# A graph network's passage from its first layers to its third: late adjacency slabs behind the last row, their indices apart, and another first node tile

## The chip, the core and the metric

The kernel runs on one core of a Trainium2 chip. The core has five engines with an instruction queue each: TensorE (PE) for matmuls, VectorE (DVE), ScalarE (ACT), GpSimd (POOL, which here issues mostly indirect gathers) and SyncE (SP, which here issues most of the DMAs). Within a queue the order is fixed; between queues, semaphores hold an instruction until what it needs is there. The metric is the time of one execution in microseconds (us), lower is better; the median of several runs is compared.

## What is computed

There are N = 2708 nodes with D = 512 features each and a sparse 2708 x 2708 adjacency with values. Four layers follow each other, each a normalization (subtract the mean, divide by the deviation), a Relu, a graph operation and a residual addition:

```
x = x + L0(relu(norm(x)), adj)   # inc = adj + (adj>0)/|row|;  inc @ h / row sum of inc
x = x + L1(relu(norm(x)), adj)   # 8-head attention, scores - 1e16 * (1 - max(adj, I)), softmax
x = x + L2(relu(norm(x)), adj)   # relu(adj @ (h W1) + b1); relu(adj @ (. W3) + b3); tanh(. Wf + bf)
x = x + L3(relu(norm(x)), adj)   # mean of (h W + b) over the nonzero neighbours
```

The term of 1e16 in layer 1 outweighs the scores, so the softmax picks the neighbour with the largest value in the row of `max(adj, I)`. The kernel uses this: with y = relu(norm(x)) Wv Wo for all nodes, layer 1 is a gather of one row of y per node. It checks by flags that this holds, and has a general path behind them for the case that it doesn't.

## The kernel before

Nodes are handled in 22 tiles of 128 rows (the last has 20). A stretch of 128 rows of the adjacency, 128 x 2708 floats or 1354 KB, is called a slab.

**Layer 0** loops over row tiles m = 0 to 21. A row's sum (`acc`, L810) has a dense part over the first six column tiles (`inc`, made on VectorE in L641 and L649) and a listed part: nonzero rows found by a search, gathered by POOL (L580, L599) and multiplied chunk by chunk (`incl`). VectorE adds the sum to x (`xt`, L826), then come the statistics and the normalization (`norm`, ending in `shift`, L183, and a ScalarE pass `hn`, L186). For layer 1, TensorE transposes `hn` (L192) one row later and multiplies it by the joined weights (`yacc`, L158) two rows later; ScalarE copies the product to `yo` (L756) and SP stores it to `y` (L758).

Beside that each slab goes through passes of its own. On ScalarE: a sign pass and a Relu pass (L527, L528 for late slabs) that count entries. On VectorE, in `attended`: the maximum with the identity (L567), MAX8 (L568) and FIND_INDEX8 (L569), which give the index of the largest entry, `at_top`. The slabs have a ring of three buffers. Six of the slabs, the tiles 3, 4, 5, 0, 1, 2 in this order (`LATE`), are loaded at the start for the row norms alone and loaded again from row m = 14 on, one per row (`load_slab`, L521); their passes follow one row later (`count_signs`, `attended`). A 1x1 copy (`behind`, L164) ties each late sign pass to the row's `xt`.

Ranks of nonzeros for the tiles 1 and 2 are worked out late too: a scan, a store `rank_b` (L387), loads `ranks` (L404), four searches `found` (L420); `ends` (L414) waits for such a load.

After the last row come the copy `idx` of all indices (L861), `degrees` (18 short loads of counts on SP, L338, and 22 short list matmuls, L324), the last two tiles' y and the flags.

**Layer 2** begins with two bias loads (L1072) and `fetch` for the first nine tiles: a load of x into a slot (L1086, SP) and a gather of y by `idx` into another slot (L1088, POOL). Then W3, loaded before, is split into three parts on ScalarE and VectorE (`wb`, L197 to L207), and Wf is loaded (L170). The first output row's loop takes the node tiles 0, 1, 2, ... in order: add the two slots (L1100), store x2 (L1101), normalize, transpose (L923), multiply by W1 (L948), and use the product in the row's own sum (L1032 for the six dense tiles, L1047 for the others).

The order on each engine is not the program's order: a list scheduler with a cost model of its own places the instructions. `issue_after` orders one instruction behind another in that placing, and is no wait on the chip. Memory pools of layer 0 are released before layer 2's are opened, and layer 2's tiles lie over them.

Of the kernel before, what the change touches and what calls it, by code (L numbers as in the profile page):

```python
# [42 lines left out]
def kernel(  # L43
# [92 lines left out]
    idx = const.tile([P, NT], U32, name="idx")  # L136
    BAD_NEG, BAD_MANY, BAD_BOUND = NT, 2 * NT, 3 * NT
    bad = const.tile([P, 3 * NT + 1], FP, name="bad")
    nc.gpsimd.memset(bad, 0.0)
    flag = const.tile([P, 1], I32, name="flag")  # L140
# [32 lines left out]
    def norm(pool, xt, n, dst, func=AF.Identity):  # L173
# [9 lines left out]
        nc.vector.tensor_scalar(  # L183
            shift[:n], mv[:n, 0:1], rstd[:n], -1.0, op0=ALU.mult, op1=ALU.mult
        )
        nc.scalar.activation(dst[:n], xt[:n], func, scale=rstd[:n], bias=shift[:n])  # L186

    def transpose_relu(psum, hn, n, dst):
# [4 lines left out]
        nc.scalar.activation(dst, pt[:, :, :n], AF.Relu)  # L193
# [32 lines left out]
    with tc.tile_pool(name="l0_slab", bufs=2) as slabs, tc.tile_pool(  # L226
# [286 lines left out]
        LATE = FIRST + ZERO  # L513
# [9 lines left out]
        def count_signs(m, last):  # L523

            sgn = slabs.tile([P, N], BF, name="sgn", bufs=GROUP)
            behind(sgn[:1, :1], last)
            nc.scalar.activation(sgn, slab[m], AF.Sign, accum_out=sums_sgn[:, m : m + 1])  # L527
            nc.scalar.activation(sgn, sgn, AF.Relu, accum_out=cnts[:, m : m + 1])  # L528
# [215 lines left out]

        def after(m, hn):

            n = rows(m)
            if hn is not None:
                hTs[m] = wp.tile([P, NCD, P], FP, name="hT")
                transpose_relu(ps_tr, hn, n, hTs[m][:, :, :n])  # L750
                return
# [4 lines left out]
            nc.scalar.copy(yo[:n], yacc[:n])  # L756
# [43 lines left out]
        for m in range(NT):  # L800
# [29 lines left out]
            norm(wp, xt, n, hns[m])  # L830
# [6 lines left out]
            step = m - (NT - 8)  # L837
            if 0 <= step < len(LATE):
                load_slab(LATE[step])
            if 0 < step <= len(LATE):  # L840
                count_signs(LATE[step - 1], xt[:1, :1])
                attended(LATE[step - 1])
# [18 lines left out]
        nc.vector.tensor_copy(idx, at_top[:, :, 0])  # L861
        degrees()
        after(NT - 2, None)
        after(NT - 1, hns.pop(NT - 1))
        after(NT - 1, None)
        flush()
        flags()
# [7 lines left out]

    gp = short.enter_context(tc.tile_pool(name="g", bufs=1))
    wsetb = short.enter_context(tc.tile_pool(name="wsetb", bufs=1))
# [82 lines left out]
    if TAIL:  # L960
        others.append([NFULL])

# [28 lines left out]
    def aggregate(m, parts, shifted, gd, marked):  # L991
# [18 lines left out]
        for ts in dense if dense_of(m) else []:  # L1010
# [13 lines left out]
            for i, t in enumerate(ts):  # L1024
                ghi, glo, gs_ = gs[i]
                first, last = t == 0, t == DENSE - 1
                for acc, a, b, st, sp in (
                    (main, hi, ghi, first, False),
                    (main, lo, glo, False, last),
                    (mixed, s, gs_, first, False),  # L1030
# [789 lines left out]
```

## Time and profile before

| | |
|---|---|
| median of three runs | 1399.31 us (1396.03 to 1404.63) |
| profiled execution | 1402.48 us |
| its span | 1400.7 us |
| mean TensorE clock granted | 0.962 |
| TensorE busy | 1278.7 us (91%) |
| VectorE busy | 932.4 us (67%) |
| ScalarE busy | 689.2 us (49%) |
| POOL busy | 662.4 us (47%) |
| bytes moved | 348.35 MB, mean 249 GB/s |
| loads of slabs | 27, 1354 KB each |
| MAX8 over a slab (L568) | 22, 2.97 us each |
| sign pass of a late slab (L527) | 6, 2.45 us each |

Layer 0 ends and layer 2 begins at about 420 to 490 us of the span. In rows of the trace, the first number is the start, the second the duration, then engine, line, operation, and output <- input; in brackets stands how long the engine was idle before it and what is taken to have ended that. SPq is SP's queue of DMA issues. In the page's rows of 40 digits each digit is the busy share of 35 us in tenths. The rows of a table by windows give start and end, the window's length, then the busy time of PE, PEld (weight loads), DVE, ACT and POOL, the granted clock, the DMA share and GB/s.

### The profile page before, as it was taken

The page shows a single profiled execution, that of the slowest core. Times are in us where ns is not written, and L with a number is a line of the kernel's source. Part 1 is how long each engine was busy: PE and PEld are TensorE (multiplying, and loading weights), DVE is VectorE, ACT ScalarE, POOL GpSimd, SP SyncE. Part 2 cuts the span into 40 slices and gives each one's busy share as a digit, 9 for nine tenths or more (in the row PEclk, how much of TensorE's full clock was granted, in tenths as well). Part 3 has the DMA queues.
Part 4 walks back from the last instruction along what each step waited for, and adds up shares of the span by engine and source line. Part 5 has one row for each costly group of instructions (what it writes and reads, how often), then busy time and mean ns, then how long its engine had stood idle before and what let it go on. Part 6 is the DMA issues. An engine that isn't in the chain of part 4 may idle for free.

```text
span 1400.7 us, 15489 instructions
## 1 busy us (share of the span) xinstructions
PE 1278.7 (91%) x4478; PEld 770.3 (55%) x4478; DVE 932.4 (67%) x1760; ACT 689.2 (49%) x1051; POOL 662.4 (47%) x702
## 2 busy tenths in 40 slices
PE   4889989988887489899999999899999999968997
PEld 2334434434333267556656666466666666646886
DVE  4788999987797688533434446365566656657786
ACT  5887735832444465422333335244455544555553
POOL 2256477778754311265444441333334344635762
PEclk9999999999998799999999999899999999999999
DMA  9999999997884875477777767756555665748994
GB/s 343 359 323 324 316 345 350 318 375 261 295 304 120 306 257 173 161 260 256 247 211 238 239 222 227 240 173 195 170 164 172 197 202 187 243 147 287 301 278 161
DMA packets 188461, 348.35 MB, mean 249 GB/s; under 512 B 22174, under 2 KB 98868, under 8 KB 184636
## 3 DMA queue, kind: packets, MB, share of 16 engines
q1 hardware_dynamic: 140768, 200.13, 42.4%
q0 software_dynamic: 46032, 145.05, 32.1%
q10 hardware_dynamic: 1568, 2.10, 0.4%
q8 instruction: 37, 0.61, 0.2%
q14 instruction: 56, 0.46, 0.1%
HBM read 284.59 MB, written 62.61 MB: 248 GB/s over the span
## 4 chain that ended last, share of the span: by engine, by line
PE 63%; DMA 17%; DVE 9%; issue 4%; ACT 3%; POOL 2%; SPq 0%; DVEq 0%; ACTq 0%; POOLq 0%
PE aggs L1035 15%; PE main L948 10%; PE agg L1032 8%; PE acc L810 6%; DMA h<-h0d,idx_g 5%; PE mixed L948 4%; PE aggs L1032 4%; PE agg L1223 3%; PE aggs L1223 3%; PE pt L923 3%; PE yacc L158 2%; PE aggs L1047 2%; DVE found L420 1%; PE pt L1223 1%; DMA wa<-in_L_gnn_Wo_dram 1%
## 5 line engine op out<-in xcount | busy, mean ns | idle before, releaser
L1035 PE MATMUL aggs<-gg,ac 128*128 128x512 f32 (+1 forms) x520 | 232.4, 594 | 4.3 <-DMA gg<-g1d,idx_g 4.3
L983 POOL DMA_INDIRECT gg<-g2d,idx_g x130 | 131.1, 1009 | 220.5 <-PE aggs L1035 172.0
L983 POOL DMA_INDIRECT gg<-g1d,idx_g x130 | 133.8, 1029 | 173.9 <-PE aggs L1035 103.3
L810 PE MATMUL acc<-h,inc 128*128 128x512 f32 (+1 forms) x348 | 166.5, 629 | 21.2 <-DVE inc L649 21.2
L580 POOL DMA_INDIRECT ac<-in_adj_t_dram,idx_a x130 | 139.2, 1071 | 62.2 <-issue 32.6
L1035 PEld LDWEIGHTS aggs<-gg,ac 128*128 128x128 f32 (+1 forms) x520 | 97.5, 189 | 111.4 <-issue 101.4
L599 POOL DMA_INDIRECT h<-h0d,idx_g x111 | 112.0, 1009 | 56.0 <-issue 38.8
L810 PEld LDWEIGHTS acc<-h,inc 128*128 128x128 f32 (+1 forms) x348 | 67.2, 200 | 103.8 <-issue 77.2
L1019 ACT ACTIVATE a_hi<-raw 128x384 fp32r<-128x384 f32 x84 | 43.5, 520 | 160.9 <-issue 87.8
L1032 PE MATMUL agg<-ghi,a_hi 128*128 128x512 f32 x252 | 115.2, 457 | 1.8 <-ACT a_hi L1019 1.6
L810 PE MATMUL acc<-h,incl 128*128 128x512 f32 (+1 forms) x222 | 104.7, 618 | 8.2 <-DMA h<-h0d,idx_g 8.2
L1032 PE MATMUL agg<-glo,a_lo 128*128 128x512 f32 x252 | 101.9, 404 | 2.4 <-ACT glo L207 2.4
L1032 PE MATMUL aggs<-gs,a_s 128*128 128x512 f32 x252 | 100.4, 401 | 1.1 <-DVE gs L204 1.0
L1020 DVE TENSOR_TENSOR a_lo<-raw,a_hi 128x384 fp32r<-128x384 f32 x84 | 47.3, 563 | 78.4 <-ACT a_hi L1019 50.8
L929 DVE SCALAR_TENSOR_TENSOR v_lo<-pt,v_hi 128x512 fp32r<-128x512 f32 (+1 forms) x88 | 56.7, 665 | 45.2 <-ACT v_hi L928 44.6
L158 PE MATMUL yacc<-wvo,hT 128*128 128x512 f32 (+1 forms) x176 | 82.8, 611 | 1.7 <-ACT hT L193 1.7
L983 POOL DMA_INDIRECT gg<-hidr,idx_h x62 | 62.5, 1009 | 42.8 <-PE aggs L1223 18.2
L910 DVE SCALAR_TENSOR_TENSOR u<-aggs,u 128x512 f32<-128x512 f32 x42 | 28.9, 687 | 76.5 <-PE aggs L1035 75.0
L810 PEld LDWEIGHTS acc<-h,incl 128*128 128x128 f32 (+1 forms) x222 | 41.3, 196 | 57.3 <-issue 39.6
L928 ACT ACTIVATE v_hi<-pt 128x512 fp32r<-128x512 f32 (+1 forms) x88 | 48.6, 578 | 44.1 <-PE pt L923 42.2
L180 ACT ACTIVATE rstd<-mv,eps 128x1 f32<-128x1 f32 x88 | 24.5, 290 | 86.9 <-DVE mv L178 45.3
L568 DVE MAX8 tops<-ar 128x8 f32<-128x2708 f32 (+1 forms) x22 | 65.4, 2972 | 0.1
(326 smaller groups left out, 2787.3 us busy)
## 6 DMA issues: line engine op xcount, KB each, us to landing
ar<-in_adj_dram SPq DMA_DIRECT2D x27, 1354.0 KB
raw<-in_adj_t_dram SPq DMA_DIRECT2D x122, 192.0 KB
slot<-x SPq DMA_DIRECT2D x41, 256.0 KB
at<-in_adj_t_dram SPq DMA_DIRECT2D x27, 384.0 KB
ranks<-rank_b SPq DMA_DIRECT2D x20, 485.2 KB
ac<-lst SPq DMA_DIRECT2D x16, 384.0 KB
h<-in_x_dram SPq DMA_DIRECT2D x21, 256.0 KB
h0d<-h POOLq DMA_DIRECT2D x21, 256.0 KB
```

Of the source, the lines that this page charges most:

```text
L158: nc.tensor.matmul(acc[:n], hT[:, c, :n], w[:, c, :], start=(c == 0), stop=(c == NCD - 1))
L568: nc.vector.max(tops[:n, m, :], ar[:n])
L580: nc.gpsimd.indirect_dma_start(out=ac[:, c, :n], out_offset=None, in_=adj_units, element_offset=dense_of(m) * P * N + m * P, in_offset=bas ...
L599: nc.gpsimd.indirect_dma_start(out=g, out_offset=None, in_=h0d[:, :], in_offset=bass.IndirectOffsetOnAxis(ap=idx_g[:, m, c : c + 1], axis=0),)
L810: product = nc.tensor.matmul(acc[:n], a, g, start=(i == 0), stop=(i == len(pairs) - 1))
L928: nc.scalar.activation(hi[d], pt[d], AF.Relu, scale=UP)
L929: nc.vector.scalar_tensor_tensor(lo[d], pt[d], 0.0, hi[d].bitcast(FP), op0=ALU.max, op1=ALU.subtract)
L948: nc.tensor.matmul(acc[:n], a[:, c, :n], b[:, c, :], start=first and c == 0, stop=last and c == NCD - 1,)
L983: nc.gpsimd.indirect_dma_start(out=gs[c], out_offset=None, in_=gd[:, :], in_offset=bass.IndirectOffsetOnAxis(ap=index[:, m, c : c + 1], ax ...
L1032: nc.tensor.matmul(acc[:n], a[:k, i, :n], b[:k], start=st, stop=sp)
L1035: nc.tensor.matmul(mixed[:n], a, g, start=(c == 0 and not dense_of(m)), stop=(c == len(chunks) - 1),)
L1223: nc.tensor.matmul(bank_h(m)[: rows(m)], a, b, start=(i == 1), stop=(i == total))
```

## The change

Slab 0 leaves the late list: it goes through its Relu pass and `attended` at its first load at the start, and is not loaded again. Slabs 3 and 4 keep their places in rows 15 and 16, without the 1x1 copies. Slab 5 is loaded in row 18, its ScalarE passes are in row 19; slabs 1 and 2 are loaded in rows 19 and 20. The passes of these three on VectorE, and slab 2's on ScalarE, stand behind the last row's normalization and the last `yo`. The copy of indices is split: `idx` from tile 3 on, behind slab 1's pass in the program, and that of tiles 0 to 2, in a tile of its own, `idx_late`, at the end. `degrees` moves to row 18. In layer 2 the first row takes the node tiles 3 to 11, then 0 to 2, then the rest; slots are numbered by that order; W3's split and Wf's load stand in the program behind the tenth tile; the biases and the g parts get memory pools of their own, opened in another order.

```diff
-        LATE = FIRST + ZERO
+        LATE = FIRST + ZERO[1:]
...
-        def count_signs(m, last):
+        def sign_pass(m):
 
             sgn = slabs.tile([P, N], BF, name="sgn", bufs=GROUP)
-            behind(sgn[:1, :1], last)
             nc.scalar.activation(sgn, slab[m], AF.Sign, accum_out=sums_sgn[:, m : m + 1])
+            late_signs[m] = sgn
+
+        late_signs = {}
+
+        def relu_pass(m):
+
+            sgn = late_signs.pop(m)
             nc.scalar.activation(sgn, sgn, AF.Relu, accum_out=cnts[:, m : m + 1])
...
-            step = m - (NT - 8)
-            if 0 <= step < len(LATE):
-                load_slab(LATE[step])
-            if 0 < step <= len(LATE):
-                count_signs(LATE[step - 1], xt[:1, :1])
-                attended(LATE[step - 1])
+            if m == NT - 4:
+                degrees()
+            for i, t in enumerate(LATE):
+                if m == (NT - 8 + i if i < 2 else NT - 6 + i):
+                    load_slab(t)
+                if i < 2 and m == NT - 7 + i:
+                    with tc.issue_after(last_v), tc.issue_after(last_s):
+                        sign_pass(t)
+                        relu_pass(t)
+                        attended(t)
+                if i == 2 and m == NT - 3:
+                    with tc.issue_after(last_s):
+                        sign_pass(t)
+                        relu_pass(t)
...
         flush()
-        nc.vector.tensor_copy(idx, at_top[:, :, 0])
-        degrees()
         after(NT - 2, None)
+        with tc.issue_after(last_hT[0]):
+            sign_pass(LATE[3])
         after(NT - 1, hns.pop(NT - 1))
+        with tc.issue_after(last_hT[0]):
+            relu_pass(LATE[3])
         after(NT - 1, None)
         flush()
-        flags()
...
+        with tc.issue_after(last_v), tc.issue_after(last_yo[0]):
+            attended(LATE[2])
+            nc.vector.tensor_copy(idx[:, LEAD:], at_top[:, LEAD:, 0])
+            attended(LATE[3])
+            sign_pass(LATE[4])
+            relu_pass(LATE[4])
+            attended(LATE[4])
+            nc.vector.tensor_copy(idx_late, at_top[:, :LEAD, 0])
+            flags()
...
+    wsetb = short.enter_context(tc.tile_pool(name="wsetb", bufs=1))
+    gq = short.enter_context(tc.tile_pool(name="gq", bufs=1))
     gp = short.enter_context(tc.tile_pool(name="g", bufs=1))
-    wsetb = short.enter_context(tc.tile_pool(name="wsetb", bufs=1))
+    biases = short.enter_context(tc.tile_pool(name="biases", bufs=1))
...
+    pieces_1 = dense[1:] + others[:2] + dense[:1] + others[2:]
...
-            in_offset=bass.IndirectOffsetOnAxis(ap=idx[:n, t : t + 1], axis=0),
+            in_offset=bass.IndirectOffsetOnAxis(
+                ap=(idx_late if t < LEAD else idx)[:n, t : t + 1], axis=0
+            ),
...
-        if t + AHEAD < NT:
-            fetch(t + AHEAD)
+        for k in order_1[order_1.index(t) + AHEAD :][:1]:
+            fetch(k)
+        if t == order_1[AHEAD]:
+            w3.extend(split_w(wsetb, wr, "wb"))
+            wr = load_w(wset, wf_d, "wr")
...
-    for t in range(min(AHEAD, NT)):
+    for t in order_1[:AHEAD]:
         fetch(t)
-    w3 = split_w(wsetb, wr, "wb")
-    wr = load_w(wset, wf_d, "wr")
+    w3 = []
```

## The prediction

> **What bounds the kernel now.** I read the page first: engine rows in 40 slices of 35 us, then the chain by engine.
>
> ```profile
> PE   4889989988887489899999999899999999968997
> DVE  4788999987797688533434446365566656657786
> PE 63%; DMA 17%; DVE 9%; issue 4%; ACT 3%; POOL 2%; SPq 0%; DVEq 0%; ACTq 0%; POOLq 0%
> ```
>
> TensorE carries the span except in two dips. The first (digits 7 and 4, about 420 to 490 us) is the passage from layer 0 to layer 2; the change works there and at the start. In layer 0, ahead of it, VectorE stands at 7 to 9. The chain over 360 to 560 us says who holds the passage:
>
> ```profile
> 421.94 2.98 DVE tops L568
> 430.83 2.56 ACT sgn L527 x2
> 433.78 2.94 DVE tops L568
> 441.80 2.56 ACT sgn L527 x2
> 444.75 2.94 DVE tops L568
> 457.51 4.11 DMA slot<-x
> 467.17 6.17 DMA slot<-y,idx
> ```
>
> Three late slabs stand in it (sign pass on ScalarE, MAX8 on VectorE), then the loads of layer 2. VectorE's order inside the rows, and what layer 2's first instructions waited for on VectorE, SP, POOL and TensorE:
>
> ```profile
> 353.14 2.98 DVE L568 MAX8 tops<-ar 128x8 f32<-128x2708 f32 x1
> 363.62 0.15 DVE L414 CAST ends<-ar 128x1 f32<-128x1 f16 x1 [7.50 <-DMA ar<-rank_l]
> 363.76 2.97 DVE L569 FIND_INDEX8 at_top<-tops,ar 128x8 uint32<-128x2708 f32 x1
> ```
> ```profile
> 444.70 2.98 DVE L568 MAX8 tops<-ar 128x8 f32<-128x2708 f32 x1
> 450.83 0.16 DVE L861 COPY idx<-at_top 128x22 uint32<-128x22 uint32 x1
> 472.26 0.69 DVE L1100 TENSOR_TENSOR slot<-slot,slot 128x512 f32<-128x512 f32 x1 [4.93 <-DMA slot<-y,idx]
> ```
> ```profile
> 461.59 0.31 SPq L758 DMA_DIRECT2D y<-yo  x1
> 462.02 0.81 SPq L1072 DMA_DIRECT2D bias<-in_L_gnn_b_dram  x2
> ```
> ```profile
> 465.70 1.17 POOL L1088 DMA_INDIRECT slot<-y,idx  x1 [11.49 <-ACT wb L207]
> ```
> ```profile
> 477.65 1.97 PE L923 MATMUL pt<-ident,slot 128*128 128x128 f32 x8 [16.74 <-ACT slot L186]
> ```
>
> The indices are ready at 451.0. The first gather starts only at 465.70, because it reads all of y, and y's last tile is stored at 461.59. (The releaser named is a weight split; I take the landing of that store, 4.1 us after its issue, since the gather reads what it writes.) The gather's rows reach the first add 6.56 us after its issue; TensorE has then been idle for 16.74 us. So the last row of y sets the start of layer 2, and the late slabs' passes, laid between the last rows' sums, set the last row of y.
>
> **The change, step by step.** Times are on the profile's own axis: span 1400.7, profiled run 1402.48 us.
>
> *One slab's passes.* On VectorE: 0.28 + 2.98 + 0.08 + 2.97, about 6.25 us. On ScalarE: sign 2.45, Relu 2.45, two reads of 0.19, 5.3 us.
>
> *Slab 0 to the start.* Removed late: 6.25 us of VectorE (around 421), 5.3 of ScalarE, one 1354 KB load. Added at the start: 6.25 us on VectorE around 25 to 32 and a Relu of 2.6 on ScalarE. The DMA share is 0.97 to 1.07 from 10 to 80 us, VectorE only 0.54 to 0.80 busy between 30 and 50; norms of h queue behind the passes, and ScalarE, 10.0 of 10 us busy from 30 to 40, gets a hole. Bounds: 8.9 us if nothing hides, -1.3 (one load of an activation table fewer, one slab reload fewer). The nearest row is the DMA share: the stage waits for bytes. I take **+1**.
>
> *Rows 17 to 21.* From the order of the changed kernel's instructions: `inc` of row 17 and `xt` of row 16 stand ahead of the `ends` that waited 7.50 us, so row 17's list is ready at about 361 instead of 369. Then slabs 5, 1 and 2 (6.25 each, before at 400, 434 and 445) and slab 0 (422) are not among the rows. A row costs TensorE 5.3 + 0.4 + 4.5 + 3.6 + 0.6 = 14.4 us (dense sum, broadcast, listed sum, y product, transposes), while before the rows' `xt` came at 369.84, 390.79, 409.05, 429.23, a period of 20. Walking each engine's order with before's durations gives `xt` of rows 17, 18, 19 at 383, 393, 413 (four searches of 2.17 us and their ranks hold row 20's list until 411.5), the last sum's end at 429 (before 439.2), the last `shift` at 431.6, and `yo` of row 21 at 443 (before 460.99). y's store lands at about 447: 18 us earlier.
>
> *The three passes behind.* They now follow the last `shift` in a line: slab 5 from 431.6 to 437.9, slab 1 to 444.4. Slab 2's MAX8 waits for its sign pass, which ScalarE runs only behind `yo` of row 21 (443 to 445.6): to 451.9. The `idx_late` copy is done at **452.3**. Its reloads (issued 405 to 420, landing by 430) are not late.
>
> *Indices apart.* By intent tiles 3 to 11 need only `idx`, complete after slab 1. But the first gather's slot and the bias tiles lie in memory released by layer 0, and in the changed program the first gather and the first bias load each still carry a wait for the `idx_late` copy and for slab 2's Relu. The nine `slot<-x` loads stand behind that bias in SP's queue, the other eight gathers behind the first on POOL. I cost the separation at nothing gained: first gather at about 452.4, against 465.70: **-13.3**.
>
> *Weight parts and biases.* Seven of the eight VectorE splits of W3 (0.64 each) still come before the first add; with the first on ScalarE at 452.4 they end at 457.7, inside the gather's 6.6 us. If the gather were faster they would bind. The 1 MB load of Wf leaves this stretch: at 350 GB/s worth up to 3 us of DMA, in which TensorE later had a 2.41 us stall behind a list load of 6.69; I take **-1**.
>
> *Transfers released together.* Eleven SP loads and nine gathers, 20 x 262 KB = 5.24 MB, start at one moment; before, five x loads had gone by 460.
>
> ```profile
> core 0: us, PE busy (x) PEld busy (x) DVE busy (x) ACT busy (x) POOL busy (x), PEclk, DMA share, GB/s
> ...
> 440.00:460.00 20.00, 13.99 (x53) 5.88 (x54) 11.20 (x38) 9.37 (x13) 9.31 (x11) 0.83 0.44 126
> 460.00:480.00 20.00, 3.26 (x12) 2.00 (x10) 12.37 (x29) 8.72 (x17) 9.73 (x10) 0.59 0.91 329
> 480.00:500.00 20.00, 16.14 (x73) 12.31 (x71) 16.29 (x36) 13.76 (x25) 5.19 (x6) 0.98 1.02 350
> ```
>
> Here a rule speaks against the change. The Trainium skill ("Trainium Kernel Development and Optimization", Key Constraints) says that transfers issued from SP, ACT and POOL share the same 16 DMA engines and interleave, so different queues bring no bandwidth. Taken to the end, all 5.24 MB land together: 15 us at 350 GB/s, first add at 467.4 instead of 472.26, gain 4.9. The row: the first gather took 6.56 us to the add with four x loads and the Wf load in flight beside it. I take the row plus **+1** for the two biases ahead of the first x load; the rule's end is a rival.
>
> *The degrees.* 18 short loads (0.28 us of issue each, 5 us) move to row 18 in SP's queue, ahead of `rank_b` and `ranks`; 22 list matmuls (0.04 us each) move into row 19. `ranks` was late at 408 before; in the walk they land at 399.6, with row 20's list behind them. Bounds 0 and +6.5 (18 loads in groups of 8 at 2.9 us); in the walk, nothing more.
>
> *First row of layer 2.* Pieces in another order, the same matmuls (two fewer or more instructions): 0. The removed 1x1 copies: six of 0.12 us, lost beside VectorE's waits.
>
> Sum: -13.3 - 1 + 1 + 1 = -12.3. Profiled 1402.48 - 12.3 = 1390.2. The median lies 3.2 below the profiled run: **1387 us**. About 1% (14 us) is what a measurement of this kernel can tell from no change.
>
> **The rivals.**
>
> *A, more (0.23).* The rows close up to TensorE's 14.4 us from row 17 on: the last `shift` comes up to 5 us earlier, and slab 2's passes with it; and the stalls of 1.03 and 2.41 us after 485 vanish. -20: 1379. For it: VectorE's idle 7.50 goes and 25 us of passes leave the rows. Against: row 20's list hangs on `ranks`, a DMA chain.
>
> *B, the transfers set the start (0.15).* The rule above: gain 4.9 at the first add, 1 lost at the start: 1395.5. For it: DMA share 1.02 from 480 to 500. Against: gathers are issued 1.25 us apart on a queue of their own.
>
> *C, slower (0.12).* The passes laid end to end, 20.7 us from the last `shift` to `idx_late`, with rows that come no earlier. Place: VectorE behind row 21. It decides from a last `shift` later than 444.9 (431.6 + 13.3). Before, the last `shift` stood at 450.9 with three passes among the rows. If the degrees' loads hold `ranks` by their full 6.5 and VectorE, the searches and the start keep the rows where they were, `shift` falls at 450, the gather at 471: +5, and the start's upper bound 8.9 on top would make +14. I put it at +6: 1405, half of its chance above 1413.
>
> That the change doesn't do what it says is in the sum already: the indices apart free no gather.
>
> **How the numbers follow.** Likeliest case 0.50, own range 1380 to 1393, 0.22 of it under 1385.3 (more than 1% faster). Faster: 0.22 + 0.23 = 0.45. Within 1%: 0.28 + 0.15 + 0.06 = 0.49. Slower by over 1%: 0.06. The range 1376 to 1402 leaves out half of C, the low end of A and little else.
>
> **What would show it.** Right: the first gather 12 to 15 us earlier, directly behind the `idx_late` copy; the last y store 5 us or more ahead of that; three MAX8/FIND_INDEX8 pairs in a row behind the last `shift`; the first add 6 to 8 us after the gather; no 7.50 wait at `ends` with a sum behind it. At the start, the first dense sums at most 1 to 2 us later. Wrong: a first gather before slab 2's MAX8 (then A or better); a last `shift` after 440 (then look at `ranks`, toward C); a first add more than 10 us after the gather (B); layer 0's rows from 60 to 350 us later by more than 3 us, which would mean that slab 0's passes weren't hidden.

## The result and the profile after

The changed kernel takes 1396.23 us (median of 20 runs, 1387.96 to 1401.22); the kernel before, beside it, 1399.97 (20 runs, 1396.03 to 1405.87). The ratio is 0.9961 with an interval of 0.9944 to 0.9979. (Medians here are of all runs, ratios of undisturbed ones alone, so that a ratio can differ from that of two medians.) It is faster by 0.4%, less than the 1% that the prediction took as the least that can be told from no change; over these runs the interval does tell it. Forecast were 1387.0, with a range of 1376 to 1402: the range held the time, the forecast itself was three times too optimistic (-12.3 against -3.7; -8.2 between the two profiled executions, 1402.48 and 1394.29).

The page of the changed kernel, TensorE, VectorE and the chain by engine:

```profile
PE   4789989996998399899999999899999999978997
DVE  4779999897896798434334445565666666658786
PE 57%; DMA 5%; ACT 2%; DVE 2%; issue 1%; POOL 1%; SPq 0%; DVEq 0%; ACTq 0%; POOLq 0%
```

The two dips of TensorE at the passage (7 and 4 before) are now nearly one (8 and 3): the wait has been gathered in one place. A new one has come, a 6 at 315 to 350 us, where there was an 8; it is row 14, below. The chain over 360 to 560 us names what stands in it:

```profile
440.16 2.45 ACT sgn L529 x2
...
444.77 3.62 PE yacc L159 x8
449.00 2.46 ACT sgn L529 x2
451.81 2.98 DVE tops L577
454.87 3.01 DVE at_top L578 x2
460.45 1.10 SPq L1135
462.47 9.86 DMA slot<-x
```

On VectorE only slab 2's passes are still in it, and they stand behind the last product of y (L159), as the prediction had it; on ScalarE slab 1's sign pass (440.16) stands ahead of that product. VectorE in order of time:

```profile
437.65 0.20 DVE L184 TENSOR_SCALAR shift<-mv,rstd 20x1 f32<-20x1 f32 x1
438.09 2.98 DVE L577 MAX8 tops<-ar 128x8 f32<-128x2708 f32 x1
...
444.38 2.98 DVE L577 MAX8 tops<-ar 128x8 f32<-128x2708 f32 x1
...
451.81 2.98 DVE L577 MAX8 tops<-ar 128x8 f32<-128x2708 f32 x1
...
457.91 0.17 DVE L895 COPY idx_late<-at_top 128x3 uint32<-128x3 uint32 x1
...
466.26 0.69 DVE L1152 TENSOR_TENSOR slot<-slot,slot 128x512 f32<-128x512 f32 x1 [2.76 <-DMA slot<-y,idx]
```

SP, POOL and TensorE at the beginning of layer 2:

```profile
458.63 0.81 SPq L1119 DMA_DIRECT2D bias<-in_L_gnn_b_dram  x2
```
```profile
459.02 0.99 POOL L1137 DMA_INDIRECT slot<-y,idx  x1 [9.52 <-ACT wb L200]
```
```profile
472.20 1.97 PE L954 MATMUL pt<-ident,slot 128*128 128x128 f32 x8 [23.82 <-DMA slot<-y,idx]
```

The three pairs of passes follow the last `shift` in a line, the gather starts 0.9 us after the end of the `idx_late` copy, and the first add 7.24 us behind the gather. The shape is the forecast one, but all of it comes some 5 us later than forecast (6 us, less the +1 for slab 0). Why is seen in a table of milestones, all from the two profiled executions (first transposes: TensorE's first of layer 2; first stored result: the first store to `g2d`):

| us | before | forecast | after |
|---|---|---|---|
| first `xt` (row 0) | 82.81 | +1 | 92.16 |
| `xt` of row 13 | 313.33 | +1 | 317.39 |
| `xt` of row 14 | 334.89 | +1 | 343.34 |
| last `shift` | 450.92 | 431.6 (+1) | 437.65 |
| last `shift` to end of indices | | 20.7 | 20.43 |
| first gather of y | 465.70 | 452.4 (+1) | 459.02 |
| gather to first add | 6.56 | 7.56 | 7.24 |
| first transposes of layer 2 | 477.65 | | 472.20 |
| from there to the first stored result | 119.5 | -1 | 115.1 |

Row 0 is 9.35 us late. That is the line that the prediction had named as the sign of its error ("layer 0's rows from 60 to 350 us later by more than 3 us").

One trace doesn't give the size of this delay. Eleven traces of this case have the changed kernel's start (this one and ten of the kernels below): row 0 is at 87.6 to 92.3 in them. The five without slab 0's passes at the start (before, no slab 0, the three with slab 0 late) have it at 82.6 to 83.3. The delay is 4.3 to 9.7 us, and 9.35 is near its top.

### The profile page after: what moved, and what is told of

It reads as the page before. It is cut to its first block, busy times and chain, and to the rows that moved or that the text cites. A ratio compares the mean times of both kernels' runs of the same rounds, so it can differ in the third digit from the quotient of the medians.

```text
span 1392.5 us, 15484 instructions
## 1 busy us (share of the span) xinstructions
PE 1274.6 (92%) x4478; PEld 766.2 (55%) x4478; DVE 932.2 (67%) x1754; ACT 685.2 (49%) x1048; POOL 664.6 (48%) x702
## 4 chain that ended last, share of the span: by engine, by line
PE 57%; DMA 5%; ACT 2%; DVE 2%; issue 1%; POOL 1%; SPq 0%; DVEq 0%; ACTq 0%; POOLq 0%
PE aggs L1090 15%; PE main L979 10%; PE agg L1066 8%; PE mixed L979 5%; PE aggs L1066 4%; PE agg L1277 3%; PE aggs L1277 3%; PE pt L954 3%; PE aggs L1073 2%; PE pt L1277 1%; PE agg L979 1%; DMA raw<-in_adj_t_dram 1%; DMA wb<-hid 1%; PE mixed L1277 1%; DMA slot<-x 1%
## 5 line engine op out<-in xcount | busy, mean ns | idle before, releaser
L821 PE MATMUL acc<-h,inc 128*128 128x512 f32 x348 | 164.8, 623 | 20.1 <-DVE inc L658 13.6
L589 POOL DMA_INDIRECT ac<-in_adj_t_dram,idx_a x130 | 136.0, 1046 | 52.1 <-issue 33.8
L608 POOL DMA_INDIRECT h<-h0d,idx_g x111 | 118.9, 1071 | 53.8 <-issue 39.1
L821 PEld LDWEIGHTS acc<-h,inc 128*128 128x128 f32 x348 | 65.6, 196 | 103.3 <-issue 71.8
L1066 PE MATMUL agg<-ghi,a_hi 128*128 128x512 f32 x252 | 115.2, 457 | 4.7 <-ACT a_hi L1052 4.5
L1066 PE MATMUL agg<-glo,a_lo 128*128 128x512 f32 x252 | 102.8, 408 | 0.0
L1066 PE MATMUL aggs<-gs,a_s 128*128 128x512 f32 x252 | 100.6, 402 | 0.0
L159 PE MATMUL yacc<-wvo,hT 128*128 128x512 f32 (+1 forms) x176 | 79.8, 594 | 1.2 <-ACT hT L196 1.2
L821 PEld LDWEIGHTS acc<-h,incl 128*128 128x128 f32 (+1 forms) x222 | 40.3, 193 | 53.6 <-issue 33.4
L578 DVE FIND_INDEX8 at_top<-tops,ar 128x8 uint32<-128x2708 f32 (+1 forms) x22 | 65.3, 2969 | 0.0
```

The costliest lines, as they stand in the source:

```text
L159: nc.tensor.matmul(acc[:n], hT[:, c, :n], w[:, c, :], start=(c == 0), stop=(c == NCD - 1))
L578: nc.vector.max_index(at_top[:n, m, :], tops[:n, m, :], ar[:n])
L589: nc.gpsimd.indirect_dma_start(out=ac[:, c, :n], out_offset=None, in_=adj_units, element_offset=dense_of(m) * P * N + m * P, in_offset=bas ...
L608: nc.gpsimd.indirect_dma_start(out=g, out_offset=None, in_=h0d[:, :], in_offset=bass.IndirectOffsetOnAxis(ap=idx_g[:, m, c : c + 1], axis=0),)
L821: product = nc.tensor.matmul(acc[:n], a, g, start=(i == 0), stop=(i == len(pairs) - 1))
L1066: nc.tensor.matmul(acc[:n], a[:k, i, :n], b[:k], start=st, stop=sp)
```

## The experiments

A minus or plus in a diff is against the changed kernel unless it says otherwise; "..." marks lines left out. Unless it is said, the kernel before took 1399.97 to 1400.71 us beside them.

### Is it slab 0's passes at the start?

**No passes for slab 0 at all** (its index is a constant, so node tile 0 takes a wrong row of y):

```diff
-        LATE = FIRST + ZERO[1:]
+        LATE = FIRST + ZERO[1:] + ZERO[:1]
...
-            for i, t in enumerate(LATE):
+            for i, t in enumerate(LATE[:-1]):
```


> The changed kernel with slab 0's passes (Relu, MAX8, FIND_INDEX8) left out altogether, early and late; its row of indices is preset. Theory 1 (the early passes hold the start): xt of row 0 falls from 92.2 back to 82 to 84 us, the rows up to 15 come 4 to 8 us earlier than in the changed kernel, the copy of idx_late falls from 457.9 to 450 to 454, and the time lies 4 to 7 us under the changed kernel, at 1389 to 1392. Theory 2 (the start's delay is absorbed and the missing gain lies in the tail): row 0 earlier, but idx_late within 2 us of 457.9 and the time within 2 us of the changed kernel's 1396.

Measured: 1385.96 us, ratio 0.9891 (0.9849 to 0.9933). Row 0's `xt` 83.2, last `xt` 427.8 (changed kernel 435.45), first gather 451.4.

**Slab 0 loaded again and passed late**, in rows 16 and 17, with everything else of the change kept:

```diff
...
+            if m == NT - 6:
+                load_slab(0)
+            if m == NT - 5:
+                with tc.issue_after(last_v), tc.issue_after(last_s):
+                    sign_pass(0)
+                    relu_pass(0)
+                    attended(0)
```


> The changed kernel with slab 0 late again: loaded in row 16, its passes in row 17. Theory 1: xt of row 0 at 82 to 84; rows up to 16 come 4 to 8 us earlier than in the changed kernel; row 17 and 18 lose up to 6.25 us of VectorE again; idx_late at 452 to 458, time 1390 to 1396. Theory 2: what was gained at the start is lost whole in rows 17 and 18, idx_late at 459 to 464, time 1396 to 1402.

> The changed kernel with slab 0 loaded again in row 16 and its passes in row 17, once more. If the kernel before takes about 1400 us here, both theories have it at 0.988-0.994 of that. If it takes about 1480, as in the runs after_base and the three beside it: where the start of layer 0 sets the rows also there, the time is 5 to 8 us under the 1477.7 of after_base; where other waits in the rows take that up, within 3 of it.

Measured: 1388.18 us, 0.9912 (0.988 to 0.9944), and in a later run 1390.64, 0.993 (0.9909 to 0.9951). Row 0 at 83.3 and 83.1. This kernel computes the right result and is 0.7 to 0.9% faster than the one before, where the changed one is 0.4% (the intervals touch or overlap a little).

**The early passes in the kernel before**, the one part alone (`-LATE = FIRST + ZERO`, `+LATE = FIRST + ZERO[1:]` in that kernel):

> The kernel before with slab 0's passes moved to the start and nothing else (late slabs 3, 4, 5, 1, 2 in rows 15 to 19). Theory 1: xt of row 0 at 91 to 93 as in the changed kernel, the rows 5 to 9 us late as far as row 15; one slab less in the last rows gives back up to 6.25 us; first gather at 462 to 469, time 1396 to 1404. A rival in which the delay at the start is the changed kernel's alone: xt of row 0 at 83, time 1392 to 1395.

Measured: 1409.75 us, 1.0065 (1.0047 to 1.0083), later than the theory's 1396 to 1404. Row 0's `xt` comes at 90.2, and the order at the end of layer 0 tips as well: the copies `idx_h` for layer 2 come to stand ahead of the last rows' reciprocals on VectorE. They wait 13.12 us there, for what the trace doesn't name, which holds the last y and with it the gather (465.70 before). VectorE's and POOL's timelines of this kernel:

```profile
459.21 0.17 DVE L1321 TENSOR_SCALAR idx_h<-idx_g 128x7 uint32<-128x7 uint32 x1 [13.12 <-issue]
```
```profile
477.65 1.16 POOL L1088 DMA_INDIRECT slot<-y,idx  x1 [20.38 <-DMA bias<-in_L_gnn_b_dram]
```

So this part costs in both kernels. In the changed one it is 5.6 to 8.1 us against slab 0 late (1396.23 less 1390.64 or 1388.18) and 10.3 against no passes for it at all (1385.96). The four kernels on these chips with the changed start take 1393.0 to 1397.7, the five without slab 0's passes or without its Relu at the start 1386.0 to 1390.6. In the old one the time rises by 9.0, but the last `xt` is only 3.2 later (443.56 for 440.38); the rest comes from the tipped order at the end.

### Which of the passes, and through what?

**Without the Relu pass at the start** (the count of slab 0's positive entries is then its count of entries, as for the late slabs):

```diff
-            if m in LATE:
+            if m in LATE or m == 0:
```


> The changed kernel without slab 0's Relu pass at the start (its count is taken from the sign sums, so the check of that slab's signs is left out); MAX8 and FIND_INDEX8 stay early. If ScalarE's longer queue is what delays the first sums, xt of row 0 falls by 2.6 us or more, to 86 to 89.5. If VectorE's 6.25 us ahead of the norms are, it stays at 90.5 to 92.5. Time within 3 us of the changed kernel either way.

Measured: 1389.04 us, 0.9918 (0.989 to 0.9946), row 0 at 85.5, below both forecasts. Against the changed kernel's trace that is 6.6 us. Part of it isn't the pass: the granted clock fell behind an idle time there and not here (last section), and the three traces with the changed start and no such fall have row 0 at 87.6 to 89.2. So the pass of 2.6 us on ScalarE is worth some 2 to 4 us at row 0. Nor does this run part ScalarE from VectorE, for without the Relu the scheduler placed MAX8 6 us earlier (22.35 for 28.60).

**The first normalizations of h behind slab 0's passes**, since the row sum on ScalarE had slipped from 11.30 (before) to 22.38 behind a normalization that waits 5.53 us for VectorE:

```diff
...
-        norm_h0(range(4))
+        with tc.issue_after(last_sum[0]):
+            norm_h0(range(4))
```


> The changed kernel whole, with one thing ordered: the first normalizations of h stand behind slab 0's sign pass, Relu pass and row sum on ScalarE, instead of between the sign pass and the other two. Theory 1 (the early Relu costs so much because it pushed two passes of 2.6 us out of ScalarE's idle stretch of 5.5 us into the stretch where it is never idle): xt of row 0 falls from 92.2 to 84 to 87 us, the last xt from 435.5 to 428 to 431, the time to 1388 to 1392. Theory 2 (the added work itself, 2.6 us on ScalarE and 6.25 on VectorE, is the price wherever it stands): xt of row 0 at 90 or later, time within 2 us of 1396.

Measured: 1408.52 us, 1.006 (1.0043 to 1.0077), row 0 at 93.0. The passes did run early, and nothing was gained; the theory that ScalarE's order alone is to blame falls. It isn't a pure test: the order put the very first normalization behind the row sum as well, from 19.22 to 35.08. Later rows moved too (row 13 comes at 331.7), so that the 12 us above the changed kernel aren't all from the start.

**Without the passes on VectorE** (slab 0's sign and Relu at the start kept; its index a constant):

```diff
-                if t in LATE:
+                if t in LATE or t == 0:
```


> The changed kernel with slab 0's sign and Relu passes at the start as they are, but without its passes on VectorE (maximum with the identity, MAX8, FIND_INDEX8): its index is set to a constant, so layer 1 of node tile 0 takes the wrong row and the output differs there. 6.25 us of VectorE at 28 to 35 go. Theory (VectorE's passes hold the normalizations of h, and ScalarE waits for those): xt of row 0 falls from 92.2 to 84-87 and the time by 5 or more, to 1388-1391. Rival (ScalarE's order alone: the row sum at 22.4 instead of 11.3 and a pass of 2.6 more): xt of row 0 stays at 88-92, the time at 1392-1396.

Measured: row 0 at 81.18, where the three kernels beside it that keep these passes (slab3_ahead, w3_first, pieces_orig) have it at 87.6 to 90.6. In its total, 1470.23 us, 0.9978 (0.9946 to 1.001), it can't be set beside the kernels so far: it ran on another chip, of which more below, and its profiled execution was one of its longer ones, so that only the start is read from it. The start in four kernels, by the timelines of ScalarE and of VectorE. The kernel before:

```profile
11.30 2.44 ACT L556 ACTIVATE ar<-ar 128x2708 f32<-128x2708 f32 x1
...
27.90 1.51 ACT L186 ACTIVATE h<-h,shift,rstd 128x512 f32<-128x512 f32 x2
```
```profile
26.29 0.18 DVE L181 RECIPROCAL rstd<-rstd 128x1 f32<-128x1 f32 x2
```
The changed kernel, ScalarE and VectorE:
```profile
19.22 0.81 ACT L187 ACTIVATE h<-h,shift,rstd 128x512 f32<-128x512 f32 x1 [5.53 <-DVE shift L184]
...
22.38 2.44 ACT L565 ACTIVATE ar<-ar 128x2708 f32<-128x2708 f32 x1
...
35.14 1.50 ACT L187 ACTIVATE h<-h,shift,rstd 128x512 f32<-128x512 f32 x2
```
```profile
28.60 2.98 DVE L577 MAX8 tops<-ar 128x8 f32<-128x2708 f32 x1
31.70 2.97 DVE L578 FIND_INDEX8 at_top<-tops,ar 128x8 uint32<-128x2708 f32 x1
34.65 0.20 DVE L182 RECIPROCAL rstd<-rstd 128x1 f32<-128x1 f32 x2
```
The kernel with the passes put early, ScalarE:
```profile
13.74 2.44 ACT L567 ACTIVATE ar<-ar 128x2708 f32<-128x2708 f32 x1
...
35.08 1.50 ACT L187 ACTIVATE h<-h,shift,rstd 128x512 f32<-128x512 f32 x2
```
The kernel without slab 0's passes on VectorE, ScalarE:
```profile
22.33 2.44 ACT L568 ACTIVATE ar<-ar 128x2708 f32<-128x2708 f32 x1
...
30.28 1.51 ACT L187 ACTIVATE h<-h,shift,rstd 128x512 f32<-128x512 f32 x2
```

Read the pairs. With MAX8 and FIND_INDEX8 in place, the next pair of normalizations starts at 35.1, whether the row sum on ScalarE is late (22.38) or early (13.74). Without them it starts at 30.28, with the row sum just as late. The link is in VectorE's lines: the reciprocals `rstd` that these normalizations need are a tenth or two of a us long and stand behind FIND_INDEX8, at 34.65 instead of 26.29. In the kernel without the Relu, where MAX8 stands at 22.35, the pair comes at 30.46. ScalarE normalizes h for the gathers' table and for the dense sums, and in the changed kernel TensorE's sums for row 0 wait for it:

```profile
62.29 1.98 PE L821 MATMUL acc<-h,inc 128*128 128x512 f32 x4 [1.92 <-ACT h L187]
...
73.95 3.52 PE L821 MATMUL acc<-h,inc 128*128 128x512 f32 x4 [2.20 <-ACT h L187]
```

There is a second way from VectorE to row 0, through the loads. The blocks `at` of the transposed adjacency have a ring of three buffers, and the fourth load stands in SP's queue until VectorE's `inc` has read the first block. VectorE and SP before, then in the changed kernel:

```profile
45.73 1.82 DVE L649 TENSOR_TENSOR inc<-inc,at 128x768 f32<-128x768 f32 x2
46.72 1.18 SPq L623 DMA_DIRECT2D at<-in_adj_t_dram  x2
```
```profile
48.02 0.95 DVE L658 TENSOR_TENSOR inc<-inc,at 128x768 f32<-128x768 f32 x1
49.00 2.91 SPq L632 DMA_DIRECT2D at<-in_adj_t_dram  x2
```

The load of the fifth slab stands behind them and goes out at 52.00 instead of 47.99. The DMA engines have run out of work by then; the stretch from 45 to 50 us by windows, before and after:

```profile
45.00:50.00 5.00, 4.47 (x11) 2.08 (x12) 5.00 (x10) 1.50 (x4) 0.54 (x1) 1.00 1.01 339
```
```profile
45.00:50.00 5.00, 4.45 (x11) 1.71 (x11) 4.93 (x14) 4.92 (x9) 0.54 (x1) 1.00 0.07 29
```

The DMA share falls from 1.01 to 0.07. (The fallen clock has a part in this: in the three traces without it the share is 0.59 to 0.64.) How much of the delay goes by the normalizations and how much by the loads no run here takes apart; that VectorE's two passes stand at the head of both is shown by the kernel without them (row 0 at 81.18, the fourth `at` load at 44.64).

### Row 14

Row 13 is 4 us late, row 14 more than 8. In the changed kernel slab 4's load had slipped from ahead of an x load to behind it on SP's queue (304.02 to 311.35), and the four rank stores after it took 5.41 us to issue where they took 1.22. The experiment moves slabs 3 and 4 ahead again (it is written for slab 3 alone; on SP's queue slab 4's load then comes ahead of its x load too, at 307.56 and 313.44):

```diff
+                if m == NT - 7 - 1:
+                    load_slab(LATE[0])
```


> The changed kernel with slab 3's second load written ahead of row 15's x load instead of behind it, so that on SP's queue the loads of slabs 3 and 4 come before the x loads of their rows; nothing else is altered. Theory (a slab load in front of small stores): row 14's sum is late because slab 4's 1354 KB load is issued at 311 behind an x load and the four rank stores behind it take 5 us instead of 1.2. Then row 14's xt falls from 343.3 to 336-339, the last xt from 435.5 to 430-432, the first gather from 459 to 453-455, and the time to 1390-1393. Rival (row 14 is late because everything ahead of it is late from the start): xt of row 14 stays at 342-344 and the time at 1394-1398.

> The changed kernel with the loads of slabs 3 and 4 ahead of the x loads of their rows on SP's queue. In its run slab3_ahead row 14's sum came 29.7 us behind row 13's, against 34.1 and 34.4 in the two kernels beside it that left these loads in place. Theory (the place of slab 4's load makes row 14 late): row 14 at 336-340 instead of 343, 4 us or more nearer to row 13; last xt at 430-433; time 3 to 5 us under the changed kernel's. Rival: row 14 at 342-344, time within 2 of the changed kernel's.

> The changed kernel with the loads of slabs 3 and 4 ahead of the x loads of their rows. If the kernel before takes about 1400 us here as in the first runs, the theory (the place of slab 4's load makes row 14 late, by way of the four rank stores behind it) asks for the stores' issue at 1.2-1.5 us instead of 5.41, the scan's wait of 4.83 us on VectorE gone, and xt of row 14 at 336-340 instead of 343.3, 19 to 23 us behind row 13 instead of 26. Rival: stores at 1.2-1.5 and row 14 still 25 us or more behind row 13.

The first two ran on chips where layer 0 is slower (below): 1474.01 us, 0.9934 (0.9898 to 0.9971), and 1476.64, 1.0036 (1.0006 to 1.0065). Row 14 came 29.7 and 21.3 us behind row 13 there, against 33.4 to 34.5 in the five kernels beside them without the move, which looked like a yes, but other waits lie in that stretch on those chips. The third, beside a kernel before of 1400.54, decides: 1393.0 us, 0.9946 (0.9923 to 0.9969), which can't be told from the changed kernel. Its lines, SP's and then VectorE's:

```profile
307.56 0.81 SPq L524 DMA_DIRECT2D ar<-in_adj_dram  x1
...
321.21 5.00 SPq L371 DMA_DIRECT2D rank_b<-rk  x4
```
```profile
332.34 0.85 DVE L385 TENSOR_SCALAR ar<-ar 1x2708 f16<-1x2708 bf16 x1 [5.24 <-DMA ar<-cnt_b]
```

The load is ahead (though at 307.56 still later than the 304.02 before), the stores are as slow (5.00), the wait is as long (5.24; 4.83 in the changed kernel), and row 14 comes at 342.24, 26.5 us behind row 13 (25.95). The theory that the order on the queue does it falls. What row 14 goes with is the start. In six kernels on these chips row 0 is at 82.6 to 85.5 (before, no slab 0, no Relu, and the three with slab 0 late): there the four stores take 1.2 to 1.4 us and row 14 is at 332 to 337. In six it is at 87.9 or later (the changed one, this one, the two below with the memory freed and the degrees moved, the early passes in the kernel before, and the normalizations of h behind slab 0's passes): there the stores take 4.8 to 7.3 us and row 14 is at 342 to 343, in the last one at 357.8. What makes four short stores wait there is left open.

### The tail: indices, degrees, the order on ScalarE

**Memory freed**, so that the first gather and biases no longer lie where layer 0's indices and counts were (those go to the slabs' pool, the lists to one of their own):

```diff
...
-        at_top = hp.tile([P, NT, 8], U32, name="at_top")
+        at_top = slabs.tile([P, NT, 8], U32, name="at_top", bufs=1)
...
```


> The changed kernel with the top values, indices and counts kept beside the slabs instead of beside the tiles of h, and the lists in a memory pool of their own: the first gather and the bias loads no longer wait for slab 2's passes and idx_late, only for y, idx and the last list stores. Theory 1 (that wait sets the start of layer 2): the first gather moves 4 to 6 us ahead of its place in the changed kernel, measured from the last shift, the first add stands before slab 2's FIND_INDEX8, and the time falls by 3 to 6 us, to 1390 to 1393. Theory 2 (the transfers released together set it): the gather earlier, but the first add less than 2 us earlier and the time within 2 us of 1396.

Measured: 1397.65 us, 0.998 (0.996 to 1.0001). The first gather starts at 453.65, 5.4 us earlier, ahead of the end of slab 2's passes, as the change means it. VectorE's timeline behind it:

```profile
459.11 0.69 DVE L1154 TENSOR_TENSOR slot<-slot,slot 128x512 f32<-128x512 f32 x1 [1.81 <-DMA slot<-y,idx]
459.79 2.97 DVE L580 FIND_INDEX8 at_top<-tops,ar 128x8 uint32<-128x2708 f32 x1
462.76 0.68 DVE L1154 TENSOR_TENSOR slot<-slot,slot 128x512 f32<-128x512 f32 x1
```

Neither theory holds: the first add is 7.2 us earlier (459.11, 466.26), so that the indices' memory did hold the gather, and yet the time is the same. The pass that no longer holds the gather now stands between the first two adds, TensorE waits 2.67 us ahead of a product with W1 and 2.70 us later in the row, its granted clock over the row is 0.94 (0.96 in the changed kernel), and the first result is stored at 588.8 against 587.3. Even done as meant, the separated indices gain nothing in the time.

**The degrees at their old place**, behind the last row:

```diff
-            if m == NT - 4:
-                degrees()
...
+        degrees()
```


> The changed kernel with the degrees' 18 loads and 22 list matmuls behind the last row, as before the change. If the loads ahead of the ranks cost rows 19 and 20 time, the last xt comes earlier by 1 to 6 us; if they cost nothing, as the prediction had it, the last xt stays at 435 +- 1, and the list matmuls behind the last rows cost TensorE 1 us or less ahead of the last y. Time within 3 us of the changed kernel's 1396.

Measured: 1395.08 us, 0.9949 (0.9931 to 0.9968), the same as the changed kernel. The last `xt` comes at 433.8, 1.6 us earlier, but row 13 is 1.7 earlier already (315.65). The 0 of the sum stands.

**Slab 0 late, and slab 1's Relu behind the last full `yo`** on ScalarE:

```diff
...
-        with tc.issue_after(last_hT[0]):
+        with tc.issue_after(last_hT[0]), tc.issue_after(last_yo[0]):
```


> The kernel with slab 0 late again in row 17, and slab 1's Relu pass behind yo of row 20 on ScalarE. In the run with slab 0 late, the last y product waited for that yo behind the Relu, TensorE was idle for 3.30 us and the product took 6.38 us instead of 3.6. If that order is what cost the passes behind it, the last yo comes 4 to 6 us earlier (440.5 to 442.5), the copy of idx_late at 450 to 452 instead of 455.9, and the time falls by 3 to 6 us against the run with slab 0 late, to 1383 to 1386. If slab 2's passes are held by something else (its load), idx_late stays at 454 to 456 and the time at 1388.

Measured: 1388.1 us, 0.9913 (0.9885 to 0.994), the same as with slab 0 late alone. The copy of the indices starts at 451.0, against 455.9 in the first run of that kernel but 449.8 in its second: the order on ScalarE shows no gain beyond the spread of one kernel.

### The first row of layer 2

It is 4.4 us shorter than before (119.5, 115.1) where 1 was forecast. How far single traces spread: the thirteen that leave layer 2 as changed (the one with memory freed aside) have 112.0 to 116.7; besides the kernel before, the one with the early passes in it has the old layer 2, with 117.5. Two parts of the change were put back, one at a time.

**The old order of the pieces:**

```diff
...
-    pieces_1 = dense[1:] + others[:2] + dense[:1] + others[2:]
+    pieces_1 = dense + others
```


> The changed kernel with the pieces of layer 2's row sums in their old order (six dense ones first, then the others) while the node tiles of the first row still come 3 to 11, then 0 to 2. A piece of tiles 0 to 2 is then asked for before its node tile is there. Theory (order of the pieces counts): the stretch from TensorE's first transpose to the first store of a result goes from 115.1 to 118 us or more and the time to 1398-1401. Rival (it costs nothing, as the prediction has it): 114-116 us, time within 1.5 of 1396.

> The changed kernel with the pieces of layer 2's row sums in their old order. In its run pieces_orig its first output row took 123.7 us, with waits of 1.91, 1.20, 1.43 and 2.42 us at the dense pieces, which the changed kernel doesn't have. Theory (in the old order a dense piece is multiplied right behind the product that it needs, and waits for it): 119-124 us and a time 4 to 9 us above the changed kernel's beside it. Rival (the prediction's 0): 114-116 us and within 2 us of it.

**The weight parts at their old place:**

```diff
...
-        if t == order_1[AHEAD]:
-            w3.extend(split_w(wsetb, wr, "wb"))
-            wr = load_w(wset, wf_d, "wr")
...
-    w3 = []
+    w3 = split_w(wsetb, wr, "wb")
+    wr = load_w(wset, wf_d, "wr")
```


> The changed kernel with the weight parts (W3's split into three and Wf's load) back at their old place, ahead of the first output row of layer 2. In the changed kernel the first output row, from TensorE's first transpose to the first store of a result, took 115.1 us; in the kernel before 119.6. Theory (the weight parts give these 4.5 us): the stretch goes back to 118-120 and the time to 1399-1401. Rival (the order of the pieces or of the node tiles gives them): it stays at 114-116 and the time within 1.5 of the changed kernel's 1396. The prediction's own figure for the Wf load was 1.

> The changed kernel with W3's split and Wf's load ahead of the first output row again. In its run w3_first its first output row took 117.5 us with a wait of 3.64 us at the first product with W1. Theory (the weight parts cost this row 2 to 3 us, the order of the pieces the rest): 117-118.5 us and a time 1 to 4 us above the changed kernel's. Rival (the weight parts are worth the whole 4.5): 119-120 us, 4 or more above.

And the changed kernel beside them: 

> The changed kernel once more, unaltered, as the base for the three kernels beside it: in the runs of slab3_ahead, w3_first, pieces_orig and slab0_noattend every kernel, the one before the change too, took some 80 us longer, and the changed kernel wasn't among them. Both theories: ratio 0.994-0.998 to the kernel before; from TensorE's first transpose of layer 2 to the first store of a result 114-116 us; row 14's sum 25 us or more behind row 13's.

These five ran on the two chips with a slower layer 0, so the row itself is what is compared, from the first transposes to the first stored result (in us; in each pair the second is the later run):

| | first row | median | ratio to before |
|---|---|---|---|
| changed kernel | 115.0 | 1477.70 | 1.0054 (1.0023 to 1.0084) |
| old order of pieces | 123.7, 125.3 | 1482.69, 1486.46 | 1.0041 (1.0009 to 1.0073), 1.0101 (1.0001 to 1.02) |
| weight parts ahead | 117.5, 117.5 | 1477.13, 1478.00 | 1.0009 (0.9973 to 1.0045), 1.0055 (1.0024 to 1.0086) |

TensorE's waits in the later run with the old order of the pieces, and then with the weight parts ahead:

```profile
546.10 0.50 PE L1066 MATMUL agg<-ghi,a_hi 128*128 128x512 f32 x1 [2.36 <-ACT ghi L200]
...
553.56 0.50 PE L1066 MATMUL agg<-glo,a_lo 128*128 128x512 f32 x1 [1.75 <-ACT glo L210]
...
570.00 0.79 PE L1066 MATMUL agg<-glo,a_lo 128*128 128x512 f32 x1 [2.83 <-ACT glo L210]
```
```profile
552.41 1.22 PE L979 MATMUL agg<-wa,v_hi 128*128 128x512 f32 x4 [3.83 <-ACT v_hi L959]
```

In the old order a dense piece (L1066) is multiplied right behind the product that it is made from and waits for the split of it on ScalarE and VectorE; the kernel before had two such waits, of 1.03 and 2.41 us. In the new order none is left. Putting the weight parts back costs 2.5 us of the row, the old order of the pieces 8.7 to 10.3. Of the latter, TensorE's idle time makes 4.0 to 5.1; the rest is TensorE busy for longer, at a granted clock of 0.94 instead of 0.98. The 8.7 to 10.3 isn't what the change gained: the old order of pieces was made for node tiles that begin with 0, and set against tiles that begin with 3 it waits more than it did before (this reason is argued, not shown). If the parts add up, the pieces and the tiles together gave the 2 us that the weight parts leave of the 4.4. In the totals only the pieces show, and weakly: 1486.46 (four executions, with a wide interval) against 1477.70 on the same chip; 1478.00 with the weight parts ahead is the same.

## Why the prediction was wrong in size

**Slab 0 to the start (+1): the step that failed.** The prediction weighed the bounds -1.3 and 8.9 and took +1 by the nearest row, the DMA share ("the stage waits for bytes"). The share was indeed 0.97 to 1.07 before the change, but full transfers hide VectorE's work only while the transfers don't hang on VectorE. Row 0 waits for the normalizations of h, whose reciprocals of 0.2 us stand behind a slab's 6 us on VectorE, and the loads wait for buffers that VectorE reads: after the change the share is 0.07 from 45 to 50 us. The term measured 9.35 at row 0 (4.3 to 9.7 over all traces), 4.1 at row 13, 8.45 at row 14, 6.05 at the last `shift` (437.65 against the 431.6 of the walk) and 5.6 to 8.1 in the time. The prediction had even named "norms of h queue behind the passes" and then not priced it. With this term at 0 the forecast would have been 1386, and the kernel without slab 0's passes takes 1385.96. That is luck in part: its first row of layer 2 is 6.1 us shorter than before (113.5 for 119.5), where the forecast had 1.

**The walk of rows 17 to 21, and the three passes behind: right.** In the kernel without slab 0's passes, which has the start as the walk took it, rows 17 to 19 come at 383.1, 392.8 and 410.7 for 383, 393 and 413, and the last `shift` at 430.0 for 431.6. In the changed kernel it is 20.43 us from the last `shift` to the end of the indices for 20.7, slab 2's MAX8 held by its sign pass behind the last `yo`, the first gather directly behind `idx_late`. The 6.6 us between the gather's forecast -13.3 and its -6.7 are the last `shift`'s 6.05, and some tenths.

**Indices apart (0): right**, and more than forecast: the memory does hold the gather, and freeing it brings the gather forward without a gain in the time.

**Transfers together (+1): right.** 7.24 us from gather to add. The rule of a shared pool of DMA engines, taken to its end, asked for 15. Yet it isn't idle either: over 460 to 480 us the DMA share stands at 0.97, and the chain goes through a 9.86 us load of x.

**Degrees (0): right.** **Weight parts (-1)** were about 2.5 in the row, and **pieces in another order (0)** was wrong: the count of matmuls is the same, but what each waits for isn't. Rival A let the two stalls of 1.03 and 2.41 us vanish, and so they did, but it named no cause; the diff has a likely one, the order of the pieces together with that of the node tiles.

The sum by the profile: -6.7 at the gather, +0.7 to the add, +0.6 to TensorE, -4.4 in the first row, +1.6 behind it is -8.2, as measured. So a first row better than forecast made good a part of what the start cost. The medians show -3.7, since the profiled run lies 2.5 above its median before and 1.9 below after.

## What to carry to other kernels

A short instruction that another engine waits for costs what stands ahead of it in its queue: before a long pass is moved onto an engine with idle time, list the short steps that will queue behind it and who waits for each. A stage at full DMA share is no proof that the stage hides work: look at which engine frees the buffers that the next loads wait for, and at the first row's own chain. And the order in which TensorE takes pieces has a price even when the matmuls stay the same: a piece taken right behind its making was a wait of 1.0 to 2.8 us here, one made earlier was none.

## What was not expected of the hardware

**A short idle time and half the rate.** The first line below is of the changed kernel, the second of the one with memory freed, both eight equal matmuls behind the same idle time:

```profile
37.35 6.76 PE L159 MATMUL yacc<-wa,wa 128*128 128x512 f32 x8 [2.79 <-ACT wvo L482]
```
```profile
36.79 3.70 PE L159 MATMUL yacc<-wa,wa 128*128 128x512 f32 x8 [2.79 <-ACT wvo L484]
```

The granted clock over 37 to 44 us is 0.53 in one and 1.00 in the other. In the eleven traces with the changed kernel's start, all with an idle time of 2.79 or 2.80 us there, these eight matmuls take 3.70 us in three, 5.2 to 5.4 in seven and 6.76 in one; row 0 comes at 87.6 to 89.2, at 89.8 to 92.3 and at 92.16. The Trainium skill ("TensorE: Matmul & The Clock Gate", Part 1) puts the fall to half rate behind an idle window of about 3.4 us, and the window's position by chance. The traces agree on the chance and not on the length: 2.79 us were enough.

**Other chips.** On two further chips, where slab0_noattend, slab3_ahead and slab3_ahead_b and the five kernels on the first row of layer 2 ran, the kernel before took 1481.03 and 1478.61 us. Layer 0 is some 60 us longer there, in every kernel traced, with waits that the trace can't name, such as this one of the changed kernel ahead of row 6's sum:

```profile
233.08 0.75 DVE L837 SCALAR_TENSOR_TENSOR xt<-acc,deg,xt 128x512 f32<-128x512 f32 x1 [25.77 <-remote]
```

There the change gains nothing: 1.0054 (1.0023 to 1.0084), with medians of all executions alike (1477.70 and 1478.61), so that a loss isn't shown either. What holds layer 0 on those chips is open.
